# Second attention by single batches on two halves of the partitions, and channel mixing of most tokens beside the last experts

## The chip, the cores and the metric

The kernel runs on one core of one Trainium2 chip. The metric is device time of one execution in microseconds (us); lower is better. Engines are named as in the profile: PE (TensorE matmuls; PEld is the loading of weights), DVE (VectorE), ACT (ScalarE), POOL (GpSimd) and SP (SyncE, whose queue issues nearly all DMAs).

## The reference, cut to what matters

The input is x of 8 batches, 512 tokens and 128 channels. Layer 0 is attention beside a state-space scan, a feed-forward part and eight experts with a shared one. Layer 1, which the change is about, is this:

```python
h = _layernorm(x) * (1 + ca) + sa
x = x + ga * attn1(h)          # val = h has shape (8, 512, 128)
h = _layernorm(x) * (1 + cb) + sb
x = x + gb * ffn1(h)

# attn1: seq_len, bsz = 8, 512
q = (swapaxes(val, 0, 1) @ Wq.T + bq) * scale      # (512, 8, 128); k and v alike
mq = swapaxes(q.reshape(8, 512, heads, d), 0, 1)   # 8 heads of 16
# each of 512 rows: 8 queries, 8 keys and 57 zero keys, softmax, times values
out = swapaxes(attn, 0, 1).reshape(8, 512, 128)

# ffn1: x_prev is x one token earlier, zero ahead of the first
r = sigmoid((mu_r * x + (1 - mu_r) * x_prev) @ W_r.T)
k = square(relu((mu_k * x + (1 - mu_k) * x_prev) @ W_k.T))
out = r * (k @ W_v.T)
```

The reshape mixes tokens and batches. With token t = 64 i + u of batch s, attention runs over the eight groups i for fixed u and s. What comes out for group i, row u and batch s is added to batch i, token 8 u + s. So batch s of the second attention feeds each output batch in every eighth token, and an output batch is complete only when all eight have been through. The mixing of token 8 u + s needs the token before it, which is from batch s - 1, or for s = 0 from batch 7.

## The kernel before, in words

All of x is kept in SBUF as xT, channels on the partitions, 512 tokens of 8 batches along the columns. The main loop over b runs layer 0 in a software pipeline. In iteration b stand together: attention of batch b (L389 on), its state-space scan (ssm_scan), the head of batch b + 1 (load and two layernorms), the inputs of its scan, and finish(b - 1), which is the tail (layernorm, feed-forward, layernorm, routing) and nine experts of the batch before. Each is a generator that yields a cost after each piece, and weave (L204) takes the next piece from whichever generator has come least far; the numbers in a part are its total cost and the shares of the iteration where it begins and ends. This fixes the order of instructions on PE, ACT and DVE, which is written out (manual_schedule). POOL's and SP's orders are left to the scheduler; paced ties a piece's issue to a mark on PE's and DVE's side.

The second attention (attention2, L288) takes a pair of batches, sp. Two layernorms write hT with the tokens of group i of both batches side by side: 128 rows. For each of eight groups one matmul of 384 columns (L299) gives q, k and v, and DVE adds the biases (L306). Then, for each of eight queries, POOL multiplies 8 keys x 128 channels by it (L327, 128 x 1024) and DVE sums over a head's 16 channels (L317). After the softmax POOL multiplies the values by the weights (L364, 128 x 1024) and DVE sums over the eight keys (L357, 1.9 us). Each of eight results goes to DRAM by its own DMA (kept, L358). In the loop a pair takes two iterations: pair 0 starts at b = 3, pair 1 at b = 5, pair 2 at b = 7, 19 pieces in each iteration; pair 2 ends beside the tail and experts of batch 7. Pair 3 needs batch 7's experts and runs alone behind them.

Then kept is read back by four DMAs of 512 KB (L972), PE transposes it (L976), and DVE adds it to xT (L980, 32 times 128 x 128). Last comes mixing (L989) of each batch, in woven pairs: a layernorm (L239 mean, L241, L244 square, L249 variance, L258 the power on POOL, L263 broadcast, L270, L274), two products with the token before on POOL (L998) and DVE (L1001), three matmuls (L1007, L1011, L1017), a sigmoid, relu and square, the residual, four transposes (L1025), a copy (L1027), and the output DMA (L1028).

In an expert PE runs four matmuls of hm (L882), ACT a Silu on each (L886), PE four more (L897); DVE scales (L905) with wb, a row of weights that a DMA has spread over the partitions (L894), and POOL adds to moe (L908). Expert 0 has no weights and starts moe (L910). L912 adds moe to xT.

The lines of the functions that the change touches:

Of the kernel before, what the change touches and what calls it, by code (L numbers as in the profile page):

```python
# [72 lines left out]
def kernel(  # L73
# [63 lines left out]
    own = const.tile([P, NG + NDI * DS + 10], F32, name="own")  # L137
    qb_s = own[:, 10 : 10 + NG]
    A_sb = own[:, 10 + NG :].rearrange("p (c n) -> p c n", c=NDI)
# [96 lines left out]
    def layernorm(dst, src, scale, bias, name, lane, cost=0.9):  # L236

        mps = mm_tile(f"{name}_m")
        nc.tensor.matmul(mps, lhsT=mean_w, rhs=src, start=True, stop=True)  # L239
        d = lnp.tile([P, T], F32, tag=f"ln_d{lane}", name=f"{name}_d")  # L240
        nc.vector.tensor_sub(d, src, mps)  # L241
        yield cost
        sq = lnp.tile([P, T], F32, tag=f"ln_s{lane}", name=f"{name}_s")
        nc.scalar.activation(sq, d, AF.Square)  # L244
        yield cost

        vps = mm_tile(f"{name}_v")
        for j in range(NTT):
            nc.tensor.matmul(  # L249
                vps[:, j : j + 1],  # L250
                lhsT=sq[:, j * P : (j + 1) * P],
                rhs=mean_w[:, 0:1],
                start=True,
                stop=True,
            )
        sd = lnp.tile([P, NTT], F32, tag=f"ln_r{lane}", name=f"{name}_r")
        nc.vector.tensor_scalar(sd, vps[:, :NTT], EPS, None, ALU.add)
        nc.gpsimd.tensor_tensor(sd, sd, mhalf, ALU.pow)  # L258
        yield cost

        rps = mm_tile(f"{name}_rb")
        for j in range(NTT):
            nc.tensor.matmul(  # L263
                rps[:, j * P : (j + 1) * P],
                lhsT=sd[:, j : j + 1].to_broadcast([P, P]),
                rhs=ident,
# [3 lines left out]
        nc.vector.tensor_mul(d, d, rps)  # L270
        yield cost
        if len(dst.shape) == 3:
            d = d.rearrange("p (a b) -> p a b", a=dst.shape[1])
# [5 lines left out]

    U = T // NB  # L280
    wb_sb = const.tile([P, NWB], F32, name="wb_sb")
# [6 lines left out]
    def attention2(sp, at, nb=1):  # L288

        hT = at.tile([P, NB, 2, U], F32, tag="pr", name=f"hT{sp}", bufs=2)  # L290
        for k in range(2):
            b = 2 * sp + k
            yield from layernorm(
                hT[:, :, k, :], xT[:, b, :], mod(1, 1, b), mod(1, 0, b), f"lnc{b}", SECOND
            )
        qkv = at.tile([P, NB, 3, C], F32, tag="qkv", name=f"qkv{sp}", bufs=1)
        for i in range(NB):
            ps = mm_tile(f"qkv{sp}_{i}")
            nc.tensor.matmul(  # L299
                ps[:, : 3 * C],  # L300
                lhsT=hT[:, i, :, :].rearrange("p s u -> p (s u)"),
                rhs=cwb("qkv"),
                start=True,
                stop=True,
            )
            nc.vector.tensor_add(  # L306
                qkv[:, i, :, :].rearrange("p k c -> p (k c)"), ps[:, : 3 * C], crow("qkv_b")
            )
            yield 0.7
        yield from paced(attended(sp, at, nb, qkv))  # L310

    def attended(sp, at, nb, qkv):

        sc = at.tile([P, NB, NB, H1], F32, tag="sc", name=f"sc{sp}", bufs=1)
# [10 lines left out]
        for i in range(NB):  # L325
            pr = at.tile([P, NB, C], F32, tag="pr", name=f"pr{sp}_{i}", bufs=2)
            nc.gpsimd.tensor_mul(  # L327
                pr, qkv[:, :, 1, :], qkv[:, i, 0, :].unsqueeze(1).to_broadcast([P, NB, C])
# [4 lines left out]
            yield 0.5  # L333
# [3 lines left out]
        s3 = [P, NB, NB, H1]  # L337
        mx = at.tile([P, NB, H1], F32, tag="mx", name=f"mx{sp}", bufs=1)
# [3 lines left out]
        yield 0.5  # L342
        yield 0.5
        nc.scalar.activation(sc, sc, AF.Exp, scale=scale)
        nc.scalar.activation(mx, mx, AF.Exp, scale=-scale)
        sm = at.tile([P, NB, H1], F32, tag="sm", name=f"sm{sp}", bufs=1)
# [6 lines left out]
        kept = dram.tile([P, NB, C], F32, tag=f"ao{sp}", name=f"kept{sp}", bufs=1)  # L353
# [7 lines left out]
        for i in range(NB):  # L361
# [9 lines left out]
            last = i, pr  # L371
            yield 0.5
        gathered(last)
        at2.append(kept)


    def load_x(b):
# [791 lines left out]
```

## Time and profile before

| what | value |
| --- | --- |
| median of 3 runs | 2149.63 us (2147.32 to 2165.66) |
| the profiled execution, its own time and span | 2151.34 us, 2149.5 us |
| busy: PE, DVE, ACT, POOL | 78%, 67%, 45%, 48% of the span |
| mean granted clock of PE | 0.851 |
| end of the scan of b = 1, 2, ... 7 (L752) | 418.8, 646.9, 889.8, 1142.9, 1384.9, 1637.1, 1864.2 |
| first instruction of batch 7's tail; last expert's last matmul ends | 1899.6; 2004.5 |
| first layernorm of mixing; end | 2079.3; 2149.5 |
| L327, L364 on POOL, least and most | 2.34 to 3.33 us, 1.93 to 2.85 us |
| L317, L357, L306 on DVE, median | 1.21, 1.91, 0.55 us |
| L299 on PE, eight matmuls together at the end | 6.83 us |
| DMA from issue to landing, median: kept (64 KB), kept read back, output, weights (256 KB) | 1.6, 3.5, 2.4, 2.7 us |
| issues on SP's queue, each | 0.32 to 0.39 us |

Busy time is summed by engine and says little by itself, since the stages have different limits: a stage is read by which wait ends last in it. The cut at the end of a batch's scan is a place that each iteration passes, at 83% of it; a stage so cut holds the last 17% of one iteration and the first 83% of the next. The PE clock is the share of full speed that was granted.

### The profile page before, as it was taken

Reading aid. Unit: us, or ns where it says so; the run is one execution under the profiler, and the core shown is the slowest. Engines: PE = TensorE matmul, PEld = TensorE weight load, DVE = VectorE, ACT = ScalarE, POOL = GpSimd, SP = SyncE. Lnnn points to the kernel's source line nnn. Section 1 sums busy time; section 2 is a strip of 40 time slices with the busy share of each in tenths; the row PEclk is TensorE's granted clock in tenths of the full one; section 3 lists DMA queues with packets and bytes.
Section 4 is the critical chain, followed back from the end, with each engine's and each line's share of the span. In section 5 each row is a group of like instructions: output and inputs, shape, how many; then the busy total and the mean of one; then the engine's idle time right before and its main releaser. Section 6 shows DMA issues by size and latency. Waiting matters only on the chain. (4 is left out here: it accounts for less than half of the span.)

```text
span 2149.5 us, 22160 instructions
## 1 busy us (share of the span) xinstructions
PE 1675.3 (78%) x8408; PEld 784.4 (36%) x8408; DVE 1432.5 (67%) x1718; ACT 963.1 (45%) x1351; POOL 1022.2 (48%) x570
## 2 busy tenths in 40 slices
PE   5766788887889788877788878877787778869637
PEld 3333343333334333333333333333333334334323
DVE  2798587547863777458894677548995678425465
ACT  2522545454554455444444545453454545424113
POOL 1565345425561545246582445336573456344344
PEclk9667879988998888987898888987889879989869
DMA  2210112121322122121222122111221213103101
GB/s 98 75 69 20 60 59 99 50 65 54 104 60 70 49 74 74 40 70 45 89 68 80 37 68 89 46 64 40 79 78 46 75 64 96 50 17 102 45 20 39
DMA packets 64106, 135.79 MB, mean 63 GB/s; under 512 B 7128, under 2 KB 19552, under 8 KB 63872
## 3 DMA queue, kind: packets, MB, share of 16 engines
q1 hardware_dynamic: 63520, 132.03, 19.4%
q10 hardware_dynamic: 288, 1.93, 0.2%
q8 instruction: 66, 1.08, 0.2%
q0 software_dynamic: 192, 0.42, 0.1%
q14 instruction: 40, 0.33, 0.0%
HBM read 129.50 MB, written 4.85 MB: 63 GB/s over the span
## 5 line engine op out<-in xcount | busy, mean ns | idle before, releaser
L731 POOL TENSOR_TENSOR hs<-hs,bc 128x1024 f32<-128x1024 f32 x128 | 366.0, 2860 | 113.9 <-DVE hs L727 86.0
L727 DVE TENSOR_TENSOR_SCAN hs<-da,hs 128x512 f32<-128x512 f32 x256 | 406.2, 1589 | 4.9
L882 PE MATMUL e<-hm,we 128*128 128x512 f32 x576 | 314.1, 674 | 118.3 <-ACT eh L886 68.9
L704 POOL TENSOR_TENSOR xc<-xc,hs 128x512 f32<-128x512 f32 x112 | 181.2, 1618 | 276.9 <-DVE hs L703 276.9
L509 ACT ACTIVATE ex<-e 128x1024 f32<-128x1024 f32 (+3 forms) x256 | 165.7, 698 | 266.9 <-PE e L456 266.5
L897 PE MATMUL e<-eh,we 128*128 128x512 f32 x576 | 275.8, 623 | 0.0
L474 DVE TENSOR_REDUCE mpad<-s 128x2 f32<-128x256 f32 (+3 forms) x256 | 198.0, 815 | 96.3 <-PE s L456 95.6
L908 POOL TENSOR_TENSOR moe<-moe,wb 128x512 f32<-128x512 f32 x64 | 98.5, 1540 | 318.9 <-DVE wb L905 318.8
L886 ACT ACTIVATE eh<-e,vec_sb 128x512 f32<-128x512 f32 x288 | 186.7, 686 | 105.3 <-PE e L882 101.6
L722 DVE TENSOR_TENSOR hs<-bc,dtw 128x1024 f32<-128x1024 f32 x128 | 219.2, 1712 | 0.0
L882 PEld LDWEIGHTS e<-hm,we 128*128 128x128 f32 x576 | 109.3, 209 | 269.6 <-ACT eh L886 110.7
L448 PE MATMUL s<-kT,qT 32*128 32x128 f32 (+3 forms) x1024 | 142.0, 573 | 40.9 <-DVE kT L438 18.5
L689 ACT ACTIVATE da<-dtu,own 128x512 f32<-128x512 f32 x256 | 169.5, 715 | 0.9 <-POOL dtu L676 0.3
L448 PE MATMUL e<-qT,kT 32*128 32x512 f32 (+3 forms) x1024 | 128.7, 539 | 47.0 <-DVE qT L493 32.0
L897 PEld LDWEIGHTS e<-eh,we 128*128 128x128 f32 x576 | 111.2, 201 | 129.7 <-issue 126.3
L509 ACT ACT_TABLE_LOAD x35 | 44.9, 1283 | 174.9 <-PE e L456 174.8
L905 DVE SCALAR_TENSOR_TENSOR wb<-e,vec_sb,wb 128x512 f32<-128x512 f32 x64 | 47.8, 747 | 108.1 <-PE e L897 97.3
L520 PE MATMUL av<-ex,va 128*32 128x512 f32 (+3 forms) x1024 | 115.9, 510 | 4.0 <-ACT ex L509 3.8
L456 PEld LDWEIGHTS <-ident_b 128*128 128x128 bf16 x1024 | 64.0, 104 | 139.2 <-issue 132.3
L327 POOL TENSOR_TENSOR pr<-qkv 128x1024 f32<-128x1024 f32 x32 | 82.7, 2599 | 58.3 <-DVE sc L317 44.2
L886 ACT ACT_TABLE_LOAD x65 | 83.4, 1283 | 44.2 <-PE e L882 43.4
L703 DVE TENSOR_TENSOR hs<-hs 128x512 f32<-128x512 f32 x112 | 90.9, 812 | 16.0 <-POOL hs L731 16.0
(235 smaller groups left out, 2507.1 us busy)
## 6 DMA issues: line engine op xcount, KB each, us to landing
bc<-bc SPq DMA_DIRECT2D x128, 512.0 KB, 3.7
we<-in_w_dram SPq DMA_DIRECT2D x144, 256.0 KB, 2.7
wb<-wd SPq DMA_DIRECT2D x64, 256.0 KB, 3.3
xin<-in_x_dram SPq DMA_DIRECT2D x8, 256.0 KB, 3.4
kept<-ao SPq DMA_DIRECT2D x32, 64.0 KB, 1.6
ao<-kept SPq DMA_DIRECT2D x4, 512.0 KB, 3.5
out_dram<-xout SPq DMA_DIRECT2D x8, 256.0 KB, 2.4
wa_sb<-in_wa_dram ACTq DMA_DIRECT2D x1, 1832.0 KB
```

Source lines behind the costliest of these rows:

```text
L448: nc.tensor.matmul(tiles[i // 2][:, i % 2, :n], lhsT=lhs[quadrant(i)], rhs=rhs[quadrant(i)], start=True, stop=False,)
L474: nc.vector.tensor_reduce(mpad[:, qi, 2 * pr : 2 * pr + 2, HD : HD + 1], tiles[pr][:, :, :n], AX.X, ALU.max, negate=True,)
L509: nc.scalar.activation(t[:, :, :n], tiles[pr][:, :, :n], AF.Exp)
L520: nc.tensor.matmul(avs[g][quadrant(i), kj * P :], lhsT=va[:, kj, c0 : c0 + 32], rhs=ex[i // 2][:, i % 2, :n], start=(kj == 0), stop=(kj == ...
L689: nc.scalar.activation(da[:, n, :], dt[c], AF.Exp, scale=A_sb[:, c, n0 + n : n0 + n + 1])
L704: nc.gpsimd.tensor_add(y, y, hs[:, 0, :])
L722: nc.vector.tensor_mul(hs, bcs[0], dtx[c].unsqueeze(1).to_broadcast([P, NN, T]))
L727: nc.vector.tensor_tensor_scan(hs[:, n, :], da[:, n, :], hs[:, n, :], 0.0, ALU.mult, ALU.add)
L731: nc.gpsimd.tensor_mul(hs, hs, bcs[1])
L882: nc.tensor.matmul(ps, lhsT=we1[:, m * P : (m + 1) * P], rhs=hm, start=True, stop=True)
L886: nc.scalar.activation(t, ps, AF.Silu, bias=cv("b1", e * NFF + m))
L897: nc.tensor.matmul(ps, lhsT=we2[:, m, :], rhs=hid[m], start=(m == 0), stop=(m == NFF - 1),)
```

## The change

One batch is attended at a time. Its 64 rows stand twice on the partitions: keys and values of all eight groups on both halves, the queries of groups 0 to 3 on the lower half and of 4 to 7 on the upper. So there are four products of each kind for a batch, each as large as before. The projections become sixteen matmuls of 256 columns and eight of 128, with 64 output partitions each. Batch b - 2 is attended in iteration b, from b = 2 on; batch 6 stands beside the last tail and experts, and batch 7 behind them. The result of a batch goes to DRAM in two DMAs.

Mixing no longer waits for all of the attention. For seven of eight tokens (s below 7) attention is added and normalised for four output batches beside the last experts (SHARE = 4, in two pairs, one behind the other), and for the other four beside the attention of batch 7. Tokens with s from 1 to 6 are mixed and stored there too. Tokens with s = 7 and s = 0 of all batches are done last: closing, then closed in two halves of four batches. The sigmoid becomes a tanh, with 0.5 in the gate. Both stages use SBUF buffers of layer 0 that are free by then (tags bc0, bc1, da, hs, ex), and their own PSUM pool in place of that of the first attention. An input tile and an output tile of a mixing are the two halves of one bc0 buffer, of which there are two.

```diff
-    def layernorm(dst, src, scale, bias, name, lane, cost=0.9):
+    def normalised(src, name, lane, cost=0.9, n=T, ring=mm_tile):
...
+    def layernorm(dst, src, scale, bias, name, lane, cost=0.9, n=T, ring=mm_tile):
+        d = yield from normalised(src, name, lane, cost, n, ring)
         nc.scalar.activation(dst, d, AF.Identity, bias=bias, scale=scale)
...
-    def attention2(sp, at, nb=1):
...
+    def attention2(s, at):
+        hT = at.tile([P, 2, T], F32, tag="pr", name=f"hT{s}", bufs=2)[:, 0, :]
+        yield from layernorm(hT, xT[:, s, :], mod(1, 1, s), mod(1, 0, s), f"lnc{s}", SECOND)
...
+        for i0 in range(0, NB, 2):
+            ps = mm_tile(f"kv{s}_{i0}")
+            for i in range(2):
+                for k in range(2):
+                    nc.tensor.matmul(
+                        ps[half(k), 2 * C * i : 2 * C * (i + 1)],
+                        lhsT=hT[:, (i0 + i) * U : (i0 + i + 1) * U],
+                        rhs=cwb("qkv")[:, C:],
...
+            nc.vector.tensor_add(
+                kv[:, i0 : i0 + 2, :, :].rearrange("p i k c -> p i (k c)"),
...
+            yield 0.9
+        ps = mm_tile(f"q2{s}")
+        for i in range(NQ):
+            for k in range(2):
+                nc.tensor.matmul(
+                    ps[half(k), C * i : C * (i + 1)],
+                    lhsT=hT[:, (NQ * k + i) * U : (NQ * k + i + 1) * U],
+                    rhs=cwb("qkv")[:, :C],
...
-        for i in range(NB):
+        for i in range(NQ):
...
-            nc.sync.dma_start(out=kept[:, i, :], in_=ao)
...
+        for k in range(2):
+            nc.sync.dma_start(
+                out=kept[NQ * k : NQ * (k + 1)].rearrange("i u c -> u i c"), in_=ao[half(k)]
+            )
...
-                if b >= 3 and b % 2:
-                    second = attention2((b - 3) // 2, a2)
...
-                    parts.append((some(second, 19), 15.1 if b % 2 else 9.2, 0.0, 1.0))
+                if b >= 2:
+                    parts.append((attention2(b - 2, a2), 23.4, 0.0, 1.0))
...
-            weave((behind, 88.3, 0.0, 1.0), (second or (), 12.0, 0.0, 1.0))
...
+            banks.close()
+            pl1 = l0.enter_context(tc.tile_pool(name="pl1", bufs=5, space=PSUM))
...
+            def mixing(i, lane):
+                N = LAST * U
+                M = N - U
+                ai, o = (
+                    t.rearrange("p (j c) -> p j c", c=C)
+                    for t in halves_of(ssm, "bc0", f"ai{i}", 2)
+                )
+                for s in range(LAST):
+                    nc.sync.dma_start(out=ai[half(s % 2), s // 2, :], in_=at2[s][i])
...
+                nc.vector.scalar_tensor_tensor(
+                    xa.rearrange("p (s u) -> p s u", u=U),
+                    ps[:, :N].rearrange("p (s u) -> p s u", u=U),
+                    mod(1, 2, i),
+                    eights(i)[:, :LAST, :],
...
+                yield from layernorm(
+                    hp, xa, mod(1, 4, i), mod(1, 3, i), f"lnd{i}", lane, 0.9, N, l1_tile
+                )
+                nc.scalar.copy(x2[:, i, 1, :], xa[:, :U])
+                nc.scalar.copy(now[:, i, 1, :], hp[:, :U])
+                nc.scalar.copy(past[:, i, 0, :], hp[:, N - U :])
...
+                yield from mixed_channels(i, M, hp[:, U:], hp[:, :M], t, r)
...
+                stored(
+                    i, r, M // P, o, [rows(out[i])[:, 1 + k : LAST : 2, :] for k in range(2)]
+                )
...
+            SHARE = 4
+            weave(
+                (behind, 88.3, 0.0, 1.0),
+                (
+                    chain(
+                        attention2(LAST - 1, a2),
+                        *(pair(i, (MIX, SECOND)) for i in range(0, SHARE, 2)),
+                    ),
+                    23.4 + 11 * SHARE, 0.0, 1.0,
+                ),
+            )
...
+        weave(
+            (attention2(LAST, a2), 23.4, 0.0, 1.0),
+            (
+                chain(*(pair(i, (MIX, REST)) for i in range(SHARE, NB, 2))),
+                11 * (NB - SHARE), 0.0, 1.0,
+            ),
+        )
+        alone(closing())
+        weave((closed(0), 4.5, 0.0, 1.0), (closed(1), 4.5, 0.0, 1.0))
```

mixed_channels holds the two products with the token before, the three matmuls, relu, square and tanh; pair takes pieces of two mixings in turn; closing loads batch 7's attention, adds it, normalises and shifts by one token; closed mixes and stores.

## The prediction

> **What bounds the kernel now.** I read the slices first, then busy time by stage, with stages cut where the scan of a batch ends (L752), then the timeline of the end. In the view by stage the columns are start:end, length, busy time of PE, PEld, DVE, ACT, POOL with instructions, PE clock, DMA share, GB/s.
>
> ```profile
> 418.80:646.90 228.10, 188.78 (x991) 86.48 (x991) 149.01 (x183) 116.45 (x161) 103.68 (x56) 0.88 0.21 69
> 646.90:889.80 242.90, 202.76 (x1038) 94.54 (x1038) 155.89 (x193) 119.11 (x165) 105.00 (x58) 0.87 0.21 65
> 889.80:1142.90 253.10, 197.99 (x998) 90.33 (x997) 191.33 (x205) 117.23 (x163) 143.07 (x71) 0.84 0.19 63
> 1142.90:1384.90 242.00, 199.84 (x1038) 91.43 (x1038) 159.21 (x196) 119.23 (x165) 105.96 (x59) 0.87 0.21 66
> 1384.90:1637.10 252.20, 195.11 (x998) 89.89 (x998) 193.13 (x206) 117.45 (x163) 143.07 (x71) 0.85 0.20 62
> ...
> 1899.60:1943.00 43.40, 27.82 (x71) 14.37 (x72) 18.94 (x42) 12.37 (x17) 16.48 (x9) 0.69 0.01 4
> 1943.00:2004.50 61.50, 59.89 (x142) 25.87 (x141) 24.44 (x27) 26.32 (x39) 24.27 (x17) 1.00 0.39 116
> 2004.50:2079.30 74.80, 20.50 (x87) 13.96 (x87) 49.20 (x71) 4.95 (x7) 37.03 (x19) 0.62 0.07 25
> 2079.30:2149.50 70.20, 54.22 (x222) 29.95 (x220) 38.32 (x57) 26.11 (x41) 32.19 (x38) 0.91 0.10 30
> ```
>
> See three things. Five loop stages: the first has no second attention, the next hold a pair's projections, its scores and values, then both again; their length follows what is added, whichever engine it is for. In scores and values DVE rises by 42 (149 to 191) and the stage by 25; in projections PE rises by 14 and the stage by as much. The last batch's tail and experts (43.4 + 61.5 us): a chain of waits, then PE full (59.9 of 61.5). Last 145.0 us: attention of the last pair alone (74.8), then mixing (70.2), no engine full in the former.
>
> The timeline shows how a round through DRAM looks (columns: start, us, engine, line, operation, idle before):
>
> ```profile
> 2066.38 3.77 DVE L357 TENSOR_REDUCE ao<-pv 128x128 f32<-128x1024 f32 x2 [0.15 <-POOL pv L364]
> 2071.86 0.32 SPq L972 DMA_DIRECT2D ao<-kept  x1
> 2075.37 0.90 PE L976 MATMUL aoT<-cst_sb,ao 128*128 128x128 f32 x3 [48.79 <-DMA ao<-kept]
> ```
>
> From the last reduction's end (2070.15) to PE's transposes: 5.2 us. And PE at low and at full clock, and across changes of tile width (128*32, 32*128, 128*128):
>
> ```profile
> 1935.48 5.42 PE L882 MATMUL e<-hm,we 128*128 128x512 f32 x6
> 1942.93 3.60 PE L897 MATMUL e<-eh,we 128*128 128x512 f32 x8
> ```
> ```profile
> 1864.01 0.95 PE L538 MATMUL den<-cst_sb,at 128*128 128x4 f32 x8
> 1864.89 1.07 PE L520 MATMUL av<-ex,va 128*32 128x512 f32 x8
> 1866.76 0.93 PE L448 MATMUL e<-qT,kT 32*128 32x384 f32 x8
> 1867.62 0.40 PE L456 MATMUL e<-masks_b,ident_b 128*128 128x128 bf16 x4
> ```
>
> A pass of 512 columns costs 0.90 us cold, 0.45 warm; an f32 matmul is two passes; eight 32-wide passes take 1.07, not 3.6, so narrow tiles overlap.
>
> **The change, part by part.**
>
> *1. Loop.* Stage lengths price a pair: (242.9 + 253.1 - 2 x 228.1) = 39.8 and (242.0 + 252.2 - 456.2) = 38.0, mean 38.9, so 19.5 us a batch; projections alone 14.4 of it (mean of 14.8 and 13.9). Before, the loop held two pairs and the third's projections: 2 x 38.9 + 14.4 = 92.2. After, batches 0 to 5 at b = 2 to 7: 6 x 19.5 = 117.0. So **+25**. What a batch itself does changes: projections were eight 384-column matmuls a pair (16 passes of 0.34, so 2.7 us a batch), now sixteen of 256 and eight of 128 on 64-wide outputs: 32 x 0.225 + 16 x 0.11 = 9.0 in series, 4.5 if halves overlap (no row has 64-wide tiles; the 32-wide are nearest and overlap). DVE adds: 5 x 0.69 instead of 4 x 0.55: +1.2. Products (L327/L364) and reductions keep their sum (four of each, of the same 128 x 1024, for a batch instead of eight for a pair). Bounds for a batch: 27 (9.0 - 2.7 + 1.2 = 7.5 on top, all on the path: +70 in all) and 15 (-2 in all: values, the last 27% of a batch's pieces, fall partly behind the scan, where DVE is mostly idle: 4 x 1.91 x 0.6 = 4.6 saved). I keep 19.5: extra work and better place cancel.
>
> Rows show no gap at a change of tile width: each group above starts before the one ahead ends, so a switch costs 0. The Trainium skill, "TensorEngine Tiling (Array Packing)", Key Properties, says that changing the mode drains the array; it would speak against 64-wide matmuls put between 128-wide ones. By an estimate from "TensorE: Matmul & The Clock Gate", Single matmul latency (about 0.175 us), two switches for each of 5 pieces of 8 batches would be 14 us; the row decides for 0.
>
> *2. Last tail and experts (1899.6 to 2004.5).* It now holds attention of batch 6, then mixing of 0 and 1, then of 2 and 3. By the changed program's order on each engine:
> - Tail. Batch 6's layernorm comes ahead of ln2's on ACT and POOL: +1.5. Twelve projection matmuls stand before f2, which with q cost PE 5 or so: +6.5. pr_2 and pr_3 (POOL, 2.34 each) stand before lnb's power, and pr_1's reduction before lnb on DVE: +3. So first Silu +11 (0 if it all falls in the chain's gaps, 15 with halves in series).
> - aoT of mixing 0 stands on PE right behind expert 0 and needs batch 6's last reduction, itself behind expert 0's moe on DVE: 0.75 + 1.95 + 5.2 + 0.35 (second load) = 8.3 with PE waiting and experts 1 to 8 queued behind (0 if attention were done by then).
> - PE work of four mixings, for each: transposes 0.9, mean 0.76, variance 1.05, broadcast 1.0, three matmuls 6 x 0.33: 5.7, x4 = 22.6. PE has 1.6 us to spare in the experts, so it all counts.
> - Later waits: broadcast 1 behind POOL's moe, which waits for the first wb (wb landed 8.5 after the transposes of wT): 3; ck 0 behind wb 2 on DVE: 2.5; xa before the mean, twice: 2; power of pair 2: 1.5; mixings 2 and 3 use the buffers of 0 and 1, so their loads wait for the outputs to land: copies 1.3, issue 0.7, landing 2.4 (L1028), fourteen issues of 0.35, landing 2.1 (32 KB each; 64 KB of kept took 1.6, 256 KB of we 2.7) = 11.4 less expert 4's 3.6 and some overlap: 6.7. Sum 15.7; who waits each time is PE, and the experts behind it.
>
> Sum 11 + 8.3 + 22.6 + 15.7 = 57.6, of which I take off 3.6, since one expert group in the walk fills a wait counted twice: **+54**. Bounds: +23 (PE work alone) and +65 (15 for the tail; two gaps over 6 us, each followed by six cold passes, 2.7 dearer).
>
> Row: clock 0.69 in the stage with gaps, 1.00 in the full one. The Trainium skill, "TensorE: Matmul & The Clock Gate", What's actually happening, says an idle window of about 3.4 us halves the clock; with 5.4 us for the six cold passes behind each of two gaps this part would be +59. The row speaks for it too, but PE's gaps inside the experts are shorter than those of the tail, so I keep that in the upper bound.
>
> *3. After the last expert (t = 0).* xT of batch 7 3.0, its layernorm to hT 10.6; projections and layernorm of mixings 4 and 5 share PE to 26; POOL then runs eight ops in turn (mix, pr 2.34) to 39; scores reduced 41.6; softmax 45.7; four values 56.6. Pair 6 and 7 loads into buffers that the outputs of 4 and 5 must leave (landed 45), and its xa stands behind value 2's reduction: 54.6. A round from there takes 21 (2079.3 to 2100.8 before), output copies at 75; landing 2.4 and ai_z's load to 79.4; closing in a chain (transposes 0.6, scale and add 1.6, mean to centred 1.8, square 0.6, variance 1.3, power 1.0, broadcast 1.1, scale 0.7, two modulations 1.4, past 0.6, and 0.7 of handing over) 11.4: 90.8. The two closing halves are like the last round of before from its mix (2131.96 to 2149.5 = 17.5) plus 0.5: 108.8 against 145.0: **-36**. Bounds 95 (pair 6 and 7 starts as its loads land) and 122 (another 2.3 at each of six POOL turns): -50 to -23.
>
> *4. At nothing.* Tanh for Sigmoid: no table load between Silu and Tanh in the order; ACT works 26.3 of 61.5 there. ACT copies of 64 columns: same cover; uncovered, 24 x 0.25 = 6. SP: 31 more issues at 0.35; outside the load chains above the queue waits for buffers anyway; uncovered 11. PSUM pools swapped before the last stage: attention of batch 7, which fills the old ones, ends at 1899, when that stage begins; uncovered it is one wait of the 1.0 that its output matmul takes (L562).
>
> Sum: +25 + 54 - 36 = +43 on a span of 2149.5 and profiled time of 2151.34 (1.7 above the median 2149.63): 2194, by the median **2192**.
>
> **Rivals.**
> - *Faster: values and scores disappear in the loop.* If DVE and POOL work of a batch costs nothing beside attention, a batch is its projections, 14.4/2 = 7.2: 6 x 12.3 = 74 less: 2118. It decides below 8.8 a batch. For: DVE is busy 149 of 228. Against: pieces run from 38% to 100% of an iteration, the scan to 83%, and pairs spread alike cost 25 for scores and values.
> - *Same: the last experts take the mixing without waits.* The tail's chain has room and loads land in time, so only the 22.6 of PE remain: 31 less: 2161; below 2171 once waits shrink by 21. For: pieces of a mixing are spaced 3 us apart. Against: the order puts aoT right behind.
> - *Slower still: halves don't overlap.* 27 a batch: 6 x 7.5 = 45 more: 2237; slower by over 1% in any case, since the forecast is. For: no 64-wide row. Against: 32-wide ones overlap. This is also "the change doesn't do what it says" for the halves.
>
> **How the numbers follow.** Forecast 0.54 (own range 2172 to 2215), halves in series 0.16, PE never waits 0.18, loop hides 0.12. So faster by over 1% (below 2128) 0.12, within 1% 0.18, slower 0.70; 1% is about what a measurement can tell from none. The range leaves out the faster rival and some of the dearest: 2128 to 2240.
>
> **What would show it.** Loop stages from b = 2 on all near 248; PE idle some 8 us before the first aoT and some 6 before the third; last expert near 2230 and the rest near 109. Wrong if stages stay near 230, or if experts keep their 6.9 us pace with mixing between.

## The result and the profile after

The changed kernel takes 2155.82 us (median of 20 runs, 2149.92 to 2164.90), the kernel before 2155.19 (20 runs, 2144.20 to 2165.66): ratio 1.0011, 95% interval 0.9995 to 1.0028. No difference. The forecast was 2192, slower; the time lies in its range, but the slowdown that it forecast did not come. In the profiled executions the span went from 2149.5 to 2153.5.

Behind this zero stand three large terms. The same cuts as in the prediction, by the start of the layernorm (L242) in batch 7's tail and the end of its last expert's matmul (in expectations below, 1864 for the tail of the changed kernel is the layernorm of the second attention woven in there; the tail's own starts at 1861.8):

| stretch | before | after | measured | forecast |
| --- | --- | --- | --- | --- |
| loop, up to batch 7's tail | 1899.6 | 1861.8 | -37.8 | +25 |
| last tail and experts | 104.9 | 169.1 | +64.2 | +54 |
| behind the last expert | 145.0 | 122.6 | -22.4 | -36 |
| sum | 2149.5 | 2153.5 | +4.0 | +43 |

Busy time by stage of the changed kernel (columns as in the prediction): five stages of the loop, then tail, experts, and the rest.

```profile
414.80:649.80 235.00, 198.09 (x1058) 91.22 (x1058) 166.71 (x201) 118.79 (x165) 118.50 (x63) 0.88 0.22 66
649.80:887.40 237.60, 196.09 (x1058) 89.56 (x1057) 172.48 (x205) 118.55 (x165) 121.52 (x65) 0.90 0.22 67
887.40:1122.80 235.40, 194.13 (x1059) 88.99 (x1058) 172.61 (x205) 118.56 (x165) 121.54 (x65) 0.91 0.22 68
1122.80:1359.00 236.20, 193.89 (x1060) 88.86 (x1058) 172.54 (x205) 118.56 (x165) 121.53 (x65) 0.91 0.23 68
1359.00:1595.00 236.00, 195.74 (x1058) 89.80 (x1059) 175.07 (x206) 118.85 (x165) 121.57 (x65) 0.90 0.21 67
1861.80:1906.90 45.10, 30.44 (x129) 18.68 (x129) 17.69 (x27) 10.71 (x15) 12.78 (x8) 0.73 0.04 11
1906.90:2030.90 124.00, 98.36 (x272) 49.00 (x272) 44.29 (x80) 38.20 (x72) 25.51 (x23) 0.86 0.21 58
2030.90:2153.50 122.60, 67.17 (x236) 39.35 (x233) 62.15 (x80) 21.97 (x46) 33.56 (x27) 0.65 0.10 24
```

The loop stages are all near 236, where 248 was forecast. They hold more PE instructions than the stages of 243 to 253 before, yet PE is busy for less time (194 to 196 in the steady stages, against 195 to 203), at a higher clock (0.90 to 0.91 against 0.84 to 0.87). The expert stage now has a clock of 0.86 where it had 1.00.

The timeline of PE in the expert stage shows the waits that the second step had named (aoT is the attention that a mixing loads and PE transposes, lnd its layernorm, ck the first of its three products):

```profile
1922.39 0.49 PE L1071 MATMUL aoT<-cst_sb,ai 128*128 128x128 f32 x3
1929.83 0.37 PE L1072 MATMUL aoT<-cst_sb,ai 64*128 64x64 f32 x1 [6.95 <-DMA ai<-kept]
1930.13 0.90 PE L1071 MATMUL aoT<-cst_sb,ai 128*128 128x128 f32 x3
1931.31 1.86 PE L242 MATMUL lnd_m<-xa,cst_sb 128*128 128x448 f32 x2
1932.97 4.15 PE L918 MATMUL e<-hm,we 128*128 128x512 f32 x8
1936.96 0.92 PE L242 MATMUL lnd_m<-xa,cst_sb 128*128 128x448 f32 x2
...
1950.62 1.52 PE L270 MATMUL lnd_rb<-cst_sb,lnd_r 128*128 128x128 f32 x8 [2.19 <-POOL lnd_r L265]
1951.93 4.96 PE L933 MATMUL e<-eh,we 128*128 128x512 f32 x8
1959.79 0.91 PE L1035 MATMUL ck<-mix,wb_sb 128*128 128x384 f32 x2 [2.90 <-DVE mix L1030]
...
1961.19 3.60 PE L918 MATMUL e<-hm,we 128*128 128x512 f32 x8
...
1981.31 0.30 PE L1071 MATMUL aoT<-cst_sb,ai 128*128 128x128 f32 x1 [2.98 <-DMA ai<-kept]
1982.47 0.45 PE L1071 MATMUL aoT<-cst_sb,ai 128*128 128x128 f32 x1 [0.86 <-DMA ai<-kept]
```

The bracket is PE's idle time before the instruction and what ended it: 6.95 for the first aoT's load, 2.19 and 2.90 for broadcast and ck, and from 1978.3 on a load at a time for the third aoT, 11 us until its layernorm at 1989.1. SP's queue issues these fourteen loads one behind the other, 0.63 us apart:

```profile
1978.47 8.80 SPq L1067 DMA_DIRECT2D ai<-kept  x14
```

### The profile page after: what moved, and what is told of

It is laid out like the page before. It is cut to its first block, busy times and chain, and to the rows that moved or that the text cites. A ratio compares the mean times of both kernels' runs of the same rounds, so it can differ in the third digit from the quotient of the medians.

```text
span 2153.5 us, 22997 instructions
## 1 busy us (share of the span) xinstructions
PE 1706.0 (79%) x8762; PEld 803.1 (37%) x8762; DVE 1457.6 (68%) x1759; ACT 967.3 (45%) x1388; POOL 1001.8 (47%) x559
## 3 DMA queue, kind: packets, MB, share of 16 engines
q8 instruction: 69, 1.13, 0.2%
## 4 chain that ended last, share of the span: by engine, by line
PE 47%; DVE 32%; issue 6%; ACT 6%; POOL 5%; DMA 3%; SPq 0%; ACTq 0%; DVEq 0%; POOLq 0%
DVE hs L763 9%; PE e L933 8%; PE e L918 7%; DVE mpad L510 6%; DVE hs L758 4%; PE s L484 3%; PE e L484 3%; PE av L556 3%; POOL hs L767 2%; ACT L922 2%; PE rb L587 1%; PE q L463 1%; DVE hs L739 1%; PE s L492 1%; ACT eh L922 1%
## 5 line engine op out<-in xcount | busy, mean ns | idle before, releaser
L763 DVE TENSOR_TENSOR_SCAN hs<-da,hs 128x512 f32<-128x512 f32 x256 | 394.9, 1545 | 4.6
L740 POOL TENSOR_TENSOR xc<-xc,hs 128x512 f32<-128x512 f32 x112 | 186.0, 1660 | 271.4 <-DVE hs L739 271.4
L758 DVE TENSOR_TENSOR hs<-bc,dtw 128x1024 f32<-128x1024 f32 x128 | 213.9, 1671 | 0.0
L944 POOL TENSOR_TENSOR moe<-moe,wb 128x512 f32<-128x512 f32 x64 | 91.1, 1424 | 214.5 <-DVE wb L941 187.2
L484 PE MATMUL s<-kT,qT 32*128 32x128 f32 (+3 forms) x1024 | 140.2, 563 | 35.7 <-ACT ex L545 15.5
L394 POOL TENSOR_TENSOR pv<-kv,sc 128x1024 f32<-128x1024 f32 x32 | 61.4, 1932 | 135.8 <-DVE ao L388 114.2
L359 POOL TENSOR_TENSOR pr<-kv,q 128x1024 f32<-128x1024 f32 x32 | 92.1, 2893 | 24.8 <-DVE q L337 22.6
```

Of the source, the lines that this page charges most:

```text
L484: nc.tensor.matmul(tiles[i // 2][:, i % 2, :n], lhsT=lhs[quadrant(i)], rhs=rhs[quadrant(i)], start=True, stop=False,)
L740: nc.gpsimd.tensor_add(y, y, hs[:, 0, :])
L758: nc.vector.tensor_mul(hs, bcs[0], dtx[c].unsqueeze(1).to_broadcast([P, NN, T]))
L763: nc.vector.tensor_tensor_scan(hs[:, n, :], da[:, n, :], hs[:, n, :], 0.0, ALU.mult, ALU.add)
```

## The experiments

Two theories at first. **Evenness**: a batch's work is cheap because every iteration now has the same small share of each engine, where a pair came in lumps. **Place**: scores or values cost little because they fall behind the end of the scan (83% of the iteration), where DVE is mostly idle. A third, **form**: a batch on two halves of the partitions is cheaper in itself. Prices of a batch below are the mean of the four stages b = 3 to 6 less the 228.65 of the first run. A price comes from one profiled execution of a kernel. Five kernels here have the same loop (the changed one and the runs 13 to 16); their mean stages lie between 235.8 and 237.1, so prices that differ by about 1 us can't be told apart.

**1. No second attention in the loop.** The line that appends attention2(b - 2) is taken out; the places of the missing results are filled.

```diff
-                if b >= 2:
-                    parts.append((attention2(b - 2, a2), 23.4, 0.0, 1.0))
```

> The changed kernel with the second attention of batches 0 to 5 left out of the loop (their results are replaced by batch 6's, so the output of layer 1 is another). It gives the length of a loop stage without second attention, on which every price of a batch rests. Theory 1 (a batch is cheap when spread evenly): the base is the 228.1 us of before, stages 226 to 231, batch 7's tail starts near 1864.2 - 6 x 7.7 = 1818. Rival (the base of the changed kernel is itself lower, and a batch costs the forecast 19.5): stages 214 to 220, tail near 1747.

Stages 228.6, 228.8, 228.8, 228.4; tail at 1813.4. The base of before holds. So a batch costs (1861.8 - 1813.4) / 6 = 8.1 in the changed loop (7.7 by the four stages), and before the loop's pairs cost 1899.6 - 1813.4 = 86.2, near the 92.2 that the prediction summed for them. The pair was priced well; the single batch was not.

**2. Two batches in one iteration.**

```diff
-                if b >= 2:
-                    parts.append((attention2(b - 2, a2), 23.4, 0.0, 1.0))
+                if b >= 3 and b % 2:
+                    two = chain(attention2(b - 3, a2), attention2(b - 2, a2))
+                    parts.append((two, 46.8, 0.0, 1.0))
```

> The changed kernel, but the second attention of two batches one behind the other in the iterations 3, 5 and 7 and none in 2, 4 and 6; the work and its form are those of the changed kernel. Evenness (a lump costs, an even share does not): a loaded stage pays as a pair did before, 3 x 38.9 above the base in place of 6 x 7.7, so batch 7's tail starts near 1864.2 + 3 x 23.5 = 1935 (1910 to 1960). Form (a batch on two halves of the partitions is cheaper by itself, wherever it stands): tail within 10 of 1864. Place (values free behind the scan's end): of two batches one keeps its place, tail near 1890.

Stages 262.0, 223.3, 261.5, 223.5; tail at 1897.7: 14.0 a batch. Form alone is out: the same instructions cost 14.0 instead of 8.1. The number lies nearest to place and below what evenness gave.

**3. The kernel before, its pair divided otherwise.**

```diff
-                    parts.append((some(second, 19), 15.1 if b % 2 else 9.2, 0.0, 1.0))
+                    parts.append((some(second, 26), 18.6 if b % 2 else 5.0, 0.0, 1.0))
```

> The kernel before, a pair still over two iterations, but all scores with the projections in the odd iteration (26 pieces of cost 18.6) and only the values in the even one (5.0), so that DVE's load is shared more evenly between the two. Evenness: the stages of 243 and 253 become alike and shorter, a pair costs 20 to 30 in place of 38.9, batch 7's tail starts 10 to 35 earlier than 1899.6, the whole 2115 to 2145. Form or place: the pair keeps its price, tail within 6 of 1899.6, the whole within 10 of 2150.

2121.86 us, ratio 0.9849 (0.9809 to 0.9890). Stages 236.4, 244.7, 237.1, 240.9; tail at 1861.9, as early as the changed kernel's, in the old form. So much of the loop's gain needs no halves: the price falls from 18.9 to 11.1. It does not reach 7.7; the tail starts as early because the third pair's values now stand behind its start (112.5 for last tail and experts, 104.9 before). This speaks for evenness as it was put, but the edit also moves the scores to the last 22% of the odd iteration, behind the scan: it does not part evenness from place.

**4. Ended at 83%, with the scan.**

```diff
-                    parts.append((attention2(b - 2, a2), 23.4, 0.0, 1.0))
+                    parts.append((attention2(b - 2, a2), 23.4, 0.0, 0.83))
```

> The changed kernel with a batch's second attention ending at 0.83 of the iteration, where the scan ends, instead of at 1.0. Place (the values cost nothing because they stand behind the scan, where DVE is idle): 4 values come back among the scan's work, 4 x 1.91 and more for each of six batches, tail of batch 7 at 1880 to 1900 instead of 1864. Evenness: a little denser, tail at 1864 to 1875.

Stages 245.2, 245.2, 242.5, 243.7; tail at 1907.2. The price of a batch doubles to 15.5. Evenness is out as a rule; place gave less than this.

**5. Scores and values first, projections last.**

```diff
-                if b >= 2:
-                    parts.append((attention2(b - 2, a2), 23.4, 0.0, 1.0))
+                if b == 2:
+                    parts.append((projections2(0, a2), 9.0, 0.62, 1.0))
+                if b >= 3:
+                    two = chain(scored2(b - 3, a2), projections2(b - 2, a2))
+                    parts.append((two, 23.4, 0.0, 1.0))
```

> The changed kernel turned round in the iteration: scores and values of batch b - 3 in the first 62%, then layernorm and projections of batch b - 2. All scores and values now stand beside the scan, the projections behind it; one batch's scores and values leave the loop (batch 5's, done beside the last experts, so that stage gets longer by some 15 to 25). Place: DVE has no free place for the values any more, stages 240 to 247, tail at 1880 to 1920. Evenness (what counts is that each iteration has the same small share of each engine): stages 233 to 238, tail at 1855 to 1870.

Stages 245.9, 245.8, 245.6, 245.9; tail at 1909.1: 17.1 a batch at the same density as the changed kernel. Place is right here, evenness wrong.

**6 and 7. Begun at a quarter, and at half.** Both on the first part of the change alone (run 13 below), whose own stages are close to those of the changed kernel (236.1, 235.9, 235.8, 238.5; a price of 7.9).

```diff
-                    parts.append((attention2(b - 2, a2), 23.4, 0.0, 1.0))
+                    parts.append((attention2(b - 2, a2), 23.4, 0.25, 1.0))
```

> The first part of the change alone (2098 us, tail of batch 7 at 1867.1), with a batch's second attention begun at a quarter of the iteration instead of at its start, so that its scores stand at 54 to 77% and its values at 80 to 100%, nearly all behind the scan's end at 83%. Place: the stages fall from 236 to 230 to 234, tail of batch 7 at 1840 to 1858, the whole 2070 to 2090. Evenness: the same work in three quarters of the time is denser, stages 238 to 242, tail at 1875 to 1890, the whole 2105 to 2120.

Stages 242.4, 242.4, 242.2, 242.4; 2126.81 us, ratio 0.9851 (0.9805 to 0.9898). Values behind the scan, and the price nearly doubles to 13.7: place is refuted, and the stages lie just above what evenness gave.

> As the run before, but begun at half of the iteration: projections at 50 to 69%, scores at 69 to 84%, values at 86 to 100%. Place: scores and values cost nothing more, but the projections' 6.3 us of PE come in a fifth of the iteration where attention uses PE: stages 229 to 236. If DVE and POOL run full behind the scan: the next scan starts late, stages above 240. Evenness: twice as dense, 14 us a batch as in the run with two batches in one iteration: stages 242, tail near 1900.

The edit is the same with 0.5. Stages 232.4, 232.2, 232.1, 231.9; tail at 1844.9; 2078.09 us, ratio 0.9635 (0.9594 to 0.9676), the fastest of all. 3.5 a batch at twice the density: evenness is refuted again, and the stages are those that place gave. Neither theory survives all of these runs; the price is not a steady function of when a batch begins (0: 7.9, 0.25: 13.7, 0.5: 3.5).

Where the time goes is to be seen on PE. The same 1058 instructions, begun at a half and at a quarter (one stage each of the runs 7 and 6):

```profile
887.90:1120.10 232.20, 191.38 (x1058) 89.57 (x1058) 171.68 (x205) 118.28 (x165) 123.18 (x65) 0.90 0.21 69
```
```profile
902.60:1144.90 242.30, 198.34 (x1058) 92.40 (x1057) 174.42 (x205) 118.56 (x166) 122.85 (x65) 0.87 0.21 66
```

PE is busy 7.0 longer, at a clock of 0.87 instead of 0.90, and idle 3.1 longer (44.0 against 40.8): together the 10.1 by which the stage is longer. This divides the difference; it does not yet say what causes it. DVE and the weight loads differ by 2.7 and 2.8, ACT and POOL by less than 0.4. So the third theory: PE, the engine that is busy longest, runs in its written order and waits some 40 us in a stage; a piece put into the order costs by the waits it makes or fills and by how fast the passes around them run. The next runs ask which pieces.

**8 to 10. What in the turned order costs.** Run 5 with POOL's products left out, those of the scores (shown) and those of the values; with the reductions cut instead, the scores' to one key of eight and the values' (shown) to a copy; with both and the softmax left out.

```diff
-            nc.gpsimd.tensor_mul(
-                pr, kv[:, :, 0, :], q[:, i, :].unsqueeze(1).to_broadcast([P, NB, C])
-            )
+            pr = kv.rearrange('p j k c -> p (j k) c')[:, :NB, :]
```

> The run with scores and values first (stages 245.7, 17.1 above the base of 228.6), with POOL's eight products of a batch left out; DVE's reductions read the keys and values themselves, so the second attention computes something else. If what the scan pays is POOL's turn (a product of 1.9 to 2.9 us stands before the scan's own products on POOL's queue): stages 231 to 237. If it is DVE's (a reduction of 1.2 to 1.9 us stands before the scan on DVE's): stages 242 to 246.

Stages 244.4, 242.8, 240.6, 244.1, mean 243.0: 2.8 less. POOL's turn is not the bulk.

```diff
-            nc.vector.tensor_reduce(ao[:, i, :], pr.rearrange("p j c -> p c j"), AX.X, ALU.add)
+            nc.vector.tensor_copy(ao[:, i, :], pr[:, 0, :])
```

> The run with scores and values first (stages 245.7, 17.1 above the base), with POOL's products kept and DVE's eight large reductions of a batch cut to an eighth (only the first key enters, the other weights are zero by a small memset on POOL; the second attention computes something else). Without the products the stage fell to 241.7 on average. Theory (PE bounds the loop in its written order; a DVE instruction of 1.2 to 1.9 us that stands ahead of one that PE waits for lengthens PE's wait, and the passes behind a wait run at a low clock): stages 230 to 238. Rival (it is neither engine's work but the places of layernorm and projections on PE): stages 241 to 245.

Stages 242.8, 240.9, 240.1, 241.0, mean 241.2: 4.6 less. This misses what I expected of my theory: DVE's long instructions are not the bulk either.

```diff
-        yield from paced(attended(s, at, *projected2.pop(s)))
+        args = projected2.pop(s)
+        yield from paced(attended(s, at, *args) if s >= NB - 2 else skipped())
```

> The order with scores and values first, but with them left out and only layernorm and projections kept, at 62 to 100% of the iteration. If the 17.1 us of that order are the place of the projections: stages 240 to 246. If they are made by reductions and products beside the scan: stages 229 to 235. With the runs without products and without reductions it gives each one's share.

Stages 233.4, 237.6, 235.5, 235.6, mean 235.5: between the two expectations. Of the 17.1, layernorm and projections are 6.9, scores to values 10.3 by difference; of these, leaving out products alone gives back 2.8 and reductions alone 4.6, so neither engine's long pieces alone carry it.

**11 and 12. The batch of the changed kernel, split at its own places.**

```diff
-        yield from paced(attended(s, at, q, kv))
+        yield from paced(attended(s, at, q, kv) if s >= NB - 2 else skipped())
```

> The changed kernel with scores, softmax and values of batches 0 to 5 left out and layernorm and projections kept at their places. PE has 6.3 us of projections and 3 to 4 of layernorm in it. If prices add up and PE's work is paid in full: stages 236 to 239, at or above the 236 with everything. If PE's passes fall into its waits and keep its clock up: stages 226 to 233, and its idle time per stage below the base's 38.8 or its clock above the base's 0.87.

Stages 232.3, 231.9, 231.9, 232.4: +3.5.

```diff
+        if s < NB - 2:
...
+            for _ in range(10):
+                yield 0.9
+            yield from paced(attended(s, at, first[1], first[0]))
+            return
```

> The changed kernel with layernorm and projections of batches 0 to 5 left out and scores, softmax and values kept at their places, on constant keys, values and queries. My forecast priced them at 12.3 us a batch: stages 241. If DVE's and POOL's pieces only cost where they lie ahead of something that PE waits for: stages 229 to 236. Sum of this excess and of the run with projections only equals 7.3 if prices are additive; it misses by more than 3 if PE's projections fill waits that the scores make.

Stages 233.2, 233.6, 232.0, 232.1: +4.1 (12.3 by the forecast's share). The two sum to 7.6; together they cost 7.7. They add up. How they come about, one stage each of the run without second attention, with projections only, with scores and values only:

```profile
874.20:1103.00 228.80, 190.05 (x991) 86.74 (x992) 148.81 (x182) 116.45 (x161) 103.76 (x56) 0.87 0.22 69
```
```profile
880.80:1112.70 231.90, 196.38 (x1057) 90.98 (x1057) 151.79 (x190) 118.11 (x163) 103.56 (x57) 0.89 0.21 68
```
```profile
1111.60:1343.70 232.10, 187.05 (x994) 85.36 (x993) 166.71 (x198) 117.11 (x163) 120.20 (x64) 0.89 0.22 69
```

Projections give PE 6.3 more to do, but its idle time falls from 38.8 to 35.5: half of the work is done in waits. Scores and values let PE idle for 45.1, 6.3 more, but the same passes take 3.0 less, at a clock of 0.89 instead of 0.87. The waits of PE over two such stages name them (us in total, times, longest):

```profile
PE e L918 <- ACT eh L922: 24.8, 14, 3.2
PE e L484 <- DVE qT L529: 4.0, 6, 1.1
```
```profile
PE e L922 <- ACT eh L926: 18.4, 12, 2.6
PE e L488 <- DVE qT L533: 2.2, 2, 1.1
```
```profile
PE e L930 <- ACT eh L934: 22.2, 14, 3.2
PE e L496 <- DVE qT L541: 14.2, 6, 4.4
```

In the same order of runs: with projections the experts wait less for their Silu (24.8 to 18.4), and PE is busier there; with scores the first attention waits for the queries that DVE shifts (4.0 to 14.2). The longest of these waits has the softmax of the second attention ahead of the shift in DVE's order (DVE, then PE, in the run with scores only); in the waits of 2.1 it is a values' reduction of 1.9 that stands there.

```profile
1099.31 0.60 DVE L390 TENSOR_REDUCE sm<-sc 128x32 f32<-128x256 f32 x1
1100.03 0.76 DVE L391 SCALAR_TENSOR_TENSOR sm<-mx,sm 128x32 f32<-128x32 f32 x1
1100.82 0.35 DVE L394 RECIPROCAL sm<-sm 128x32 f32<-128x32 f32 x1
1101.20 1.15 DVE L395 TENSOR_TENSOR sc<-sc,sm 128x256 f32<-128x256 f32 x1
1102.28 0.67 DVE L541 TENSOR_TENSOR qT<-qT,mT 128x512 f32<-128x512 f32 x1
```
```profile
1103.01 1.29 PE L496 MATMUL e<-qT,kT 32*128 32x512 f32 x8 [4.43 <-DVE qT L541]
```

Loop stages of all kernels (price of a batch, mean of four stages; PE busy, idle and clock, mean of two):

| kernel | price | busy | idle | clock |
| --- | --- | --- | --- | --- |
| no second attention | 0 | 190.0 | 38.8 | 0.87 |
| projections only, scores only | 3.5, 4.1 | 196.4, 187.8 | 35.5, 45.1 | 0.89, 0.89 |
| changed kernel | 7.7 | 194.0 | 41.8 | 0.91 |
| begun at half, at a quarter | 3.5, 13.7 | 191.7, 198.2 | 40.4, 44.1 | 0.90, 0.87 |
| ended at 83%; scores first | 15.5; 17.1 | 199.9; 197.5 | 43.9; 48.2 | 0.88; 0.89 |
| old form: before; run 3 | 18.9; 11.1 | 198.9; 194.2 | 48.6; 46.7 | 0.86; 0.88 |

**13. The first part of the change alone.** Second attention by single batches; mixing of all tokens at the end as before, kept read back by two DMAs for a pair.

> The first part of the change alone: second attention by single batches in the loop, batch 6 beside the last experts, batch 7 alone behind them, then mixing of all tokens as before. If the loop's gain is the loop's own: tail of batch 7 at 1864 (as after), last tail and experts 105 + 11 to 18, then a single batch alone some 25 less than the pair's 74.8, then 70: the whole near 2105 (2090 to 2115), faster by about 2% than both kernels. If the gain is only moved (the loop ends earlier but what it left undone is paid behind it): 2135 to 2155.

2098.13 us, ratio 0.9732 (0.9696 to 0.9768). Tail at 1867.1, last tail and experts 104.3, behind them 125.3. As expected, the loop's gain is real and kept. Batch 6 beside the last experts costs no more there than the rest of a pair did (104.9), less than the 116 to 123 expected. The second part of the change gives it all back: 2153.5 - 2096.7 = 56.8.

**14 to 16. Where mixing stands.** SHARE = 0, SHARE = 2, and SHARE = 4 with an output tile of its own (a buffer of tag qT).

```diff
-            SHARE = 4
+            SHARE = 0
```

> The changed kernel with no mixing beside the last experts: all eight 7/8 mixings stand beside the attention of batch 7. By the measured parts: loop as after (tail at 1864), last tail and experts 105 + 11 to 18 instead of 166.7 (so 45 to 50 less), and behind them two more pairs of mixings, 21 to 25 each as a pair alone took, if they fit partly under the 57 of attention: 122.6 + 20 to 50. The whole 2125 to 2158. If the mixings fit wholly under the attention of batch 7: 2105.

2157.09 us, ratio 1.0009 (0.9991 to 1.0026): the upper end of what was expected. The expert stage fell further (103.3 for 116 to 123), and what lies behind grew more (184.8 for 143 to 173).

> The changed kernel with one pair of mixings beside the last experts instead of two: the second pair's waits for tiles and its 11.3 us of PE go from the experts (last tail and experts 140 to 148 instead of 166.7), and a pair is added behind them (122.6 + 10 to 25). The whole 2138 to 2152. If what bounds the stage is the number of gaps and not of mixings, the first pair keeps most of the price: 152 to 160 and 2155 to 2165.

2157.26 us in one run. Again the expert stage fell further than expected (127.6 for 140 to 148), and what lies behind grew more (158.9 for 133 to 148).

```diff
-                    for t in halves_of(ssm, "bc0", f"ai{i}", 2)
+                    for t in (
+                        ssm.tile([P, 2, T], F32, tag="bc0", name=f"ai{i}", bufs=2)[:, 0, :],
+                        act.tile([P, T], F32, tag="qT", name=f"o{i}", bufs=2),
+                    )
```

> The changed kernel with a tile of its own for what a mixing stores (a buffer of the first attention, free by then), so that the loads of the second pair don't wait for the first pair's outputs to land. By the prediction's second step the wait of the third aoT, 6.7 (about 10 as measured with the ones behind it), goes, and one cold start of the array with it: last tail and experts 169.1 less 7 to 14. Behind the last expert the same wait of the pair 6 and 7 goes: 122.6 less 3 to 12. The whole 2130 to 2145. If the loads were not what PE waits for: within 3 of 2153.

2126.55 us in one run, span 2124.8: faster than the 2130 to 2145 expected, since what lies behind fell by 21.8 where 3 to 12 was expected.

| mixing beside the last experts | last tail and experts | behind | sum |
| --- | --- | --- | --- |
| none, mixing of all tokens at the end (run 13) | 104.3 | 125.3 | 229.6 |
| none, SHARE = 0 | 103.3 | 184.8 | 288.1 |
| SHARE = 2 | 127.6 | 158.9 | 286.5 |
| SHARE = 4, the change | 169.1 | 122.6 | 291.7 |
| SHARE = 4, own output tile | 158.8 | 100.8 | 259.6 |

A pair of mixings costs 24 to 42 beside the experts and 26 to 36 behind: about the same in both places. That is dear: with all mixing at the end (run 13), PE begins a pair every 14.8 us (the transposes of the attention stand ahead of them there):

```profile
2048.78 1.88 PE L242 MATMUL lnd_m<-xT,cst_sb 128*128 128x512 f32 x4
...
2063.57 1.88 PE L242 MATMUL lnd_m<-xT,cst_sb 128*128 128x512 f32 x4
```

The shared tile costs 10.3 + 21.8 of the difference: with its own tile the third aoT follows the expert ahead of it at once (PE's timeline of run 16, then of the changed kernel behind its last expert).

```profile
1978.09 3.60 PE L933 MATMUL e<-eh,we 128*128 128x512 f32 x8
1981.53 0.49 PE L1074 MATMUL aoT<-cst_sb,ai 128*128 128x128 f32 x3
...
2053.98 0.90 PE L1051 MATMUL oT<-cst_sb,rg 128*128 128x128 f32 x3 [2.08 <-DVE rg L1094]
2054.68 0.85 PE L1074 MATMUL aoT<-cst_sb,ai 128*128 128x128 f32 x3
```
```profile
2076.52 1.11 PE L1051 MATMUL oT<-cst_sb,rg 128*128 128x128 f32 x6 [1.88 <-DVE rg L1091]
2083.46 0.45 PE L1071 MATMUL aoT<-cst_sb,ai 128*128 128x128 f32 x1 [5.84 <-DMA ai<-kept]
```

The pair 6 and 7 starts 30.7 after the last expert with its own tile, 52.6 without. Even so, 259.6 stays 30.0 above run 13. The closing and its two halves, which only the new form has, take 34.4 there from the first transposes to the end; no run takes them out, so how the 30.0 is divided stays open.

## Why the prediction was wrong

*The step that failed is the loop's price*: "Stage lengths price a pair ... so 19.5 us a batch", kept with "extra work and better place cancel". Stage and base were read rightly (228.65 measured for 228.1; 86.2 for 92.2), but a price read at the pair's places was carried to single batches at other places, as if it belonged to the work. It belongs to the place in the engines' written orders: in the new form 3.5 to 17.1 for the same instructions, 8.1 where the change puts them. That is 6 x 11.4 = 68 us against the forecast, less 6 for the old pairs: about the 62.8 by which the loop was missed, more than the whole miss of 39 in the span. That the total still fell into the range is luck: the other two steps missed by 10.2 and 13.6 the other way. The bounds (15 to 27 a batch) varied the work and let the values alone gain by their place; nothing in them let the projections fill PE's waits. The row was there: before's stages had 39 to 57 us of idle PE (length less busy) and clocks of 0.84 to 0.88, so there was room for passes to cost less than their time. Two smaller slips: "last expert near 2230" does not follow from the prediction's own sum, which puts it near 2083 (2030.9 measured); and between the second and the third of its rows on tile widths stand 32 passes of rb (1865.78 to 1866.84), with which they do follow one another without a gap.

*The rival that came nearest* is "values and scores disappear in the loop" (7.2 a batch, given 0.12). Its number fits, its mechanism does not: scores and values cost 4.1, and the projections that it paid in full cost 3.5 of 7.2.

*The halves* overlap as taken: no run shows a cost of the form. In the old form the tail starts as early too (run 3). No switch of tile width shows idle time of PE either: in the changed kernel eight projection passes of 64 outputs, 256 wide, take 1.08 us between other matmuls, where the prediction counted 1.8 in series.

*The second step* gave +64.2 for +54, inside +23 to +65 (the terms named for its upper bound add up to 63.4: 54 + 4 + 5.4). The first expert starts 9.2 later (11 forecast). The waits have about the size that was taken: first aoT 6.95 (8.3), broadcast 2.19 (3), ck 2.90 (2.5), power of the second pair 1.61 (1.5). Too small among them is the third aoT: 6.7 forecast, 7.6 of idle time measured, and 10.3 of the stage when run 16 takes its cause away. Its fourteen issues, put at 0.35 each, took 8.80 instead of 4.9. Mis-sized by more is PE's own time. Counted from the trace, the mixings' passes take 28.3 for the 22.6 forecast, and the experts' passes 69.9 where they took 65.8 before: together 9.8, about as much as the 10.2 of the miss, at a granted clock of 0.86 instead of 1.00. The Trainium skill, "TensorE: Matmul & The Clock Gate", What's actually happening, was weighed at this place (an idle window of about 3.4 us halves the clock). The wait of 6.95 does slow the passes behind it: three transposes take 0.90 instead of 0.49 ahead of it, a mean 1.86 instead of 0.92 later, the expert's eight 4.15 instead of 3.60. But behind the wait of 2.19 eight passes take 4.96, so in these rows slow passes follow a shorter wait too. The +59 that I set beside +54 went the right way; its count, two gaps with six cold passes behind each, is not what the rows show.

*The third step* gave -22.4 for -36, just outside its bounds (-50 to -23). The delay against the forecast grows on the way: 2.3 at the end of the projections, 3.5 of the scores' products, 5.1 of the softmax, 6.6 at the output copies, 8.3 at closing's transposes, 13.8 at the end. So from closing's transposes on 34.9 were taken for the 29.4 of the forecast. Part of the delay ahead of it is the contention shown last. That the loads of pair 6 and 7 waited for tiles was seen, and the bound of 95 without it is near run 16's 100.8.

What stays open: why beginning at a quarter meets worse waits than at 0 or at a half. Over two stages PE waits longer at a quarter than at a half for the experts' Silu (26.4 against 18.0) and for DVE's maxima of the first attention (12.6 against 6.9), and less for the shifted queries (4.1 against 10.3); the runs don't show which single instruction starts this. Nor does a run move one engine's order alone: a part's start and end place its pieces on PE, ACT and DVE together.

## What to carry to other kernels

A price read from a stage holds for pieces at those places in the order; before carrying it over, ask what the engine that runs through the stage does around the new places: a piece that falls in a wait is paid in part (the projections, 3.5 for 6.3 of PE's time), and one that delays what the engine waits for costs something though the engine does nothing for it (scores and values, 4.1 to 10.3). Where a weave's start and end are two numbers, try them: begun at half instead of at 0 the first part of the change went from 2098 to 2078 us with nothing else altered, and both parts of a change are worth trying alone, since here a gain of 2.7% was hidden by a loss as large. Tiles shared by input and output of a stage make each round wait for the store of the one ahead; here an own tile gave 29 us in one run.

## What the runs showed of the hardware

A DVE instruction with two tensors in SBUF that starts beside a product of 128 x 1024 on POOL lasts until that product is done. DVE's timeline, then POOL's, behind the last expert of the changed kernel; the first line is from the expert stage, with POOL idle:

```profile
2015.82 1.13 DVE L1030 SCALAR_TENSOR_TENSOR mix<-xa,vec_sb,mix 128x384 f32<-128x384 f32 x2
...
2060.38 2.70 DVE L1030 SCALAR_TENSOR_TENSOR mix<-xa,vec_sb,mix 128x384 f32<-128x384 f32 x1
2063.00 1.21 DVE L349 TENSOR_REDUCE sc<-pr 128x64 f32<-128x1024 f32 x1
2064.13 5.30 DVE L1030 SCALAR_TENSOR_TENSOR mix<-xa,vec_sb,mix 128x384 f32<-128x384 f32 x2
```
```profile
2060.02 2.64 POOL L359 TENSOR_TENSOR pr<-kv,q 128x1024 f32<-128x1024 f32 x1
2062.65 1.45 POOL L1027 TENSOR_SCALAR mix<-xa,own 128x384 f32<-128x384 f32 x2
2064.07 4.95 POOL L359 TENSOR_TENSOR pr<-kv,q 128x1024 f32<-128x1024 f32 x2
```

A mix takes 0.60 with POOL idle (1.13 for two). Started under a product of POOL it ends 0.4 behind that product, after 2.69 to 2.70, three times: 6 us more of DVE's time where the third step falls behind. The reduction with one input takes 1.21 either way (27 of 32 ran beside POOL). The Trainium skill, "SBUF — State Buffer", Who interferes with whom, says that a DVE instruction with two SBUF inputs and a GpSimd instruction that reads SBUF lock each other out and that reductions do not; the rows agree. In the loop it is there too, beside the scan's own products on POOL: of 256 scans (L763) in the changed kernel, 94 ran apart from POOL, median 1.22; the longest beside it took 3.21. It does not carry the loop's price: the 256 scans take 395.6 in the changed kernel and 394.0 without second attention in the loop (run 1).
